# Idle transposes of the identity, early transposes in pairs, and one DMA queue for the last block but one

## The chip, the cores and the metric

The kernel runs on one core of one Trainium2 chip. Time is the device time of one execution in microseconds. A core has a matrix engine (TensorE; PE in the profile, its weight loads are PEld), a vector engine (VectorE, DVE), a scalar engine (ScalarE, ACT), GpSimd (POOL) and SyncE (SP). [...] SP, ScalarE and GpSimd can issue DMA transfers; an engine that issues one is occupied for that time.

## The reference: a sandwich of attention and a feed-forward layer

The input is 1024 rows of 512 numbers, all in fp32. What is computed, with 32 query heads and 8 key-value heads (groups) of width 128:

```python
q = (hidden_states @ w_q).reshape(B, S, Hkv, g, D)
k = (hidden_states @ w_k).reshape(B, S, Hkv, D)
v = (hidden_states @ w_v).reshape(B, S, Hkv, D)
scores = jnp.einsum('bqhgd,bkhd->bhgqk', q, k) * scale
scores = jnp.where(causal, scores, -jnp.inf)
probs = jax.nn.softmax(scores.astype(jnp.float32), axis=-1).astype(q.dtype)
attn = jnp.einsum('bhgqk,bkhd->bqhgd', probs, v)
return attn.reshape(B, S, Hq * D) @ w_o
...
x = x + _layernorm(_L0_attn_ref(_layernorm(x, axis=-1), ...), axis=-1)
x = x + _layernorm(_L0_ffn_ref(_layernorm(x, axis=-1), ...), axis=-1)
```

The second layer is a dense product with a bias plus 8 low-rank experts of rank 16, weighted by a router (softmax over 15 logits, the 8 largest, mapped to experts).

## The kernel before

**Tiles.** The rows are 8 tiles of 128. Work goes by blocks: a block is one group and one tile of rows (`t`), with the group's four heads, so 64 blocks, numbered by `i`. They come in pairs of neighbouring tiles. The last two groups are interleaved at the end so that rows finish one after another and the second layer can begin; the last pair, blocks 62 and 63, is the last group with `t` = 2 and 3.

**One block.** `scores` (L350) does a block in four sub-blocks: a matmul of queries and keys into PSUM (`s`), a causal mask added by VectorE (L370), the maximum (L372, `nmax`), the exponential on ScalarE (L377, `p`), the reciprocal and the scaling (L379, L380), and a VectorE transposition of 32 x 32 pieces into a tile `T` (L383). With few keys (`t` below 4) two sub-blocks share one tile of PSUM, and the second one's matmul waits for the first one's exponential. `to_keys` (L388) then moves `T` into a tile `K` with 16 DMA transfers, which carry the probabilities to the partitions of their keys. Two blocks later `weighted_values` (L398, `po`) multiplies values by them; later still come the output projection and, for the last group, the second layer.

**Order.** TensorE's instructions and all DMA issues are pinned to program order (`keep`). So are the input's normalisations on VectorE. The others (mask, maximum, exponential, copies, the subtractions of `combine_o` on GpSimd) are placed by a planner before the program runs; every engine's order is then fixed. While a block's scores run on VectorE and ScalarE, TensorE is fed with `then`: query projections of a later pair (`pq`), products of earlier blocks (`po`), output products and second-layer pieces, cut into four shares (L701 to L704).

**Start.** The eight tiles of x and the first weights come in on SP and ScalarE's queue (L152 to L162). `input_norms` (L236) normalises each tile: statistics on VectorE, a power on GpSimd, and a scaling on VectorE (L252). `input_turn` (L260) transposes one tile with four TensorE transposes into a PSUM bank (`ptx_x`) and copies it to `xnT` on ScalarE (L234). The first four tiles are turned ahead of the blocks, with the first value projections `project_v` (`pv`) between them; `project_k` (`pk`) and `project_q` (`pq`) follow; tiles 4 and 5 are turned inside block 0, tiles 6 and 7 inside block 1. `load_o` and `combine_o` load and prepare `w_o` for group 0 on SP and GpSimd. `bank` gives one of three PSUM banks in turn to the transposes and projections.

**End.** After block 63's scores a hand-written order (L713 to L731) finishes the last four tiles of rows. It begins with the output product of blocks 60 and 61, woven with `weighted_values` of block 62.

**Queues.** `to_keys` takes the engines that issue as `by`; `two` is SP and ScalarE, `two[:1]` is SP alone. Before the change blocks 62 and 63 use both, eight transfers each:

```python
to_keys(*blocks[i], by=two if i >= N - 2 else two[:1])
```

Of the kernel before, what the change touches and what calls it, by code (L numbers as in the profile page):

```python
# [15 lines left out]
P = 128  # L16
# [6 lines left out]
def kernel(  # L23
# [37 lines left out]
    KC = H // P  # L61
    QB = 512
    NQB = S // QB
    TPB = QB // P
# [23 lines left out]
    blocks = [(g, 2 * u + e) for g, u in pairs for e in range(2)]  # L88
    N = len(blocks)
    N2 = (G - 2) * NT  # L90

    def keep(ins):
        return tc.keep_in_program_order(ins)
# [4 lines left out]
    def transpose(*args):  # L98
        keep(nc.tensor.transpose(*args))

    def load(dst, src, by=nc.sync):
        keep(by.dma_start(dst, src))

    def turn_tile(kind, g, t):

        size = (NT - 1 + t % 2) * NSUB * P
        return turn.tile([P, size], F32, tag=f"{kind}{t % 2}", name=f"{kind}_{g}_{t}")
# [39 lines left out]
    two = (nc.sync, nc.scalar)  # L147
# [16 lines left out]
    ident = const.tile([P, P], F32, tag="ident", name="ident")  # L164
# [58 lines left out]
    def bank(name):  # L223
        return ps_m.tile([P, 512], F32, tag="pm", name=name)
# [4 lines left out]
    def transposed(dst, src, name):  # L229

        pt = bank(f"ptx_{name}")
        for c in range(KC):
            transpose(pt[:, ts(c, P)], src[:, ts(c, P)], ident)
        nc.scalar.copy(dst, pt.rearrange("p (c q) -> p c q", q=P))  # L234

    def input_norms(rows):  # L236

        mvs, rstds = {}, {}

        def begin(t):  # L240
            stats = small.tile([P, 6], F32, tag="stats", name=f"stats_x{t}")
            keep(nc.vector.bn_stats(stats, x_in[:, t, :]))
            mv = mvs[t] = small.tile([P, 2], F32, tag="mv", name=f"mv_x{t}")
            keep(nc.vector.bn_aggr(mv, stats))
            ve = small.tile([P, 1], F32, tag="ve", name=f"ve_x{t}")
            keep(nc.vector.tensor_scalar(ve, mv[:, 1:2], EPS, None, ALU.add))
            rstds[t] = small.tile([P, 1], F32, tag="rstd", name=f"rstd_x{t}")
            keep(nc.gpsimd.tensor_tensor(rstds[t], ve, neg_half, ALU.pow))

        def end(t):  # L250
            row = x_in[:, t, :]
            keep(nc.vector.tensor_scalar(row, row, mvs[t][:, 0:1], rstds[t], ALU.subtract, ALU.mult))  # L252

        for n, t in enumerate(rows):
            begin(t)
            if n:
                end(rows[n - 1])
        end(rows[-1])

    def input_turn(t):  # L260
        transposed(xnT[t // TPB][:, :, ts(t % TPB, P)], x_in[:, t, :], f"x{t}")
# [3 lines left out]
    def chained(get, terms, finish, cols=512):  # L265


        pm = []

        def piece(i):  # L270
            if i == 0:
                pm.append(get())
            lhsT, rhs = terms[i]()
            matmul(pm[0], lhsT, rhs, start=(i == 0), stop=(i == len(terms) - 1))
            if i == len(terms) - 1:
                finish(pm[0])

        return [(cols, lambda i=i: piece(i)) for i in range(len(terms))]

    def project_v(gv, t):  # L280
        def finish(pm):
            v = vs[gv, t] = act.tile([P, GV * D], F32, tag="v", name=f"v_{gv}_{t}", bufs=NT + 2)
            nc.scalar.copy(v, pm)

        def term(c):
            return xnT[t // TPB][:, c, ts(t % TPB, P)], weights["v", gv, c]

        return chained(
            lambda: bank(f"pv_{gv}_{t}")[:, : GV * D],
            [lambda c=c: term(c) for c in range(KC)],  # L290
            finish,
            GV * D,
        )

    def project_k(g, qb):
        def finish(pm):
            kT = kTs[g, qb] = act.tile([P, QB], F32, tag="kT", name=f"kT_{g}_{qb}", bufs=2 * NQB)
            nc.scalar.copy(kT, pm)

        def term(c):  # L300
            return weights["k", g][:, c, :], xnT[qb][:, c, :]

        return chained(
            lambda: bank(f"pk_{g}_{qb}"), [lambda c=c: term(c) for c in range(KC)], finish
        )
# [38 lines left out]
    def turn_view(w, t):  # L344
        n = t + 1
        return w[:, : n * NSUB * P].rearrange("p (b s k q) -> p b s k q", b=R, s=NSUB, k=n)
# [41 lines left out]
    def to_keys(g, t, by=(nc.sync,)):  # L388

        src = turned.pop((g, t))  # L390
        dst = keyed[g, t] = turn_view(turn_tile("K", g, t), t)
        for h in range(R):
            for b in range(NSUB):
                load(dst[ts(b, SQ), h, :, :, :], src[ts(h, SQ), b, :, :, :], by[b % len(by)])
# [102 lines left out]
    def reload_x(t):  # L497
        xt = state["x", t] = ffn.tile([P, H], F32, tag="x", name=f"xr_{t}", bufs=1)
        load(xt, x[ts(t, P), :])
# [78 lines left out]
    def ffn_store(t):  # L578
        load(out[ts(t, P), :], acc[t])


    def projections(i):


        g, t = blocks[i]
        q, other = [], []
        m = i // 2 + 1
        if i % 2 and m < len(pairs):
            q = project_q(*pairs[m])
        if i < N2:  # L590
            if t == 2:
                other += project_k(g, 1)
            if t == 6:
                other += project_k(g + 1, 0)
            if g == 0 and t < 2:
                other += [(P * KC, lambda n=n: input_turn(n)) for n in range(TPB + 2 * t, TPB + 2 * t + 2)]
                other += project_v(0, 2 + t)
            elif g % GV == 0 and (g or t >= TPB):
                other += project_v(g // GV, t)
        else:  # L600
            n = i - N2
            for k, what in ((0, (G - 1, 0)), (2, (G - 2, 1)), (3, (G - 1, 1))):
                if n == k:
                    other += project_k(*what)
            for t in {0: (0,), 1: (1,), 2: (2, 3), 3: (4, 5), 4: (6, 7)}.get(n, ()):
                other += project_v(g // GV, t)
        return q, other

    def loads(i):

        g, t = blocks[i]
        m = (i + 1) // 2 + 1
        if i % 2 == 0 and m < len(pairs):
            for j in range(2):
                load_q(pairs[m][0], j)
        if i < N2:
            if t == 3:
                load_k(g + 1)
            if t == 5 and g + 1 == G - 2:
                load_k(G - 1)  # L620
            if t == 6 and (g + 1) % GV == 0:
                for j in range(2):
                    load_v((g + 1) // GV, j)
            if t == 5:
                load_o(g + 1)
        elif i == N2 + 3:
            load_o(G - 1)
        elif i == N2 + 4:
            load_base("wk", (0, 1))
        elif i == N2 + 5:  # L630
            load_base("wv", (2, 3))

    def run(pieces):
        for _, f in pieces:
            f()
# [23 lines left out]
    input_norms(range(TPB))  # L659
    prepare_mask()  # L660
    input_norms(range(TPB, NT))
    for t in range(TPB):
        input_turn(t)
        if t < 2:
            run(project_v(0, t))
    run(project_k(0, 0))
    run(project_q(0, 0))
    load_o(0, nc.sync)
# [2 lines left out]
    def complete(i, *behind):  # L671


        for e in range(2):
            k = i - behind[e % len(behind)]
            if 0 <= k < N and k % 2 == e and blocks[k][0] == G - 1:
                return [blocks[k][1]]
        return []

    def attend(i):  # L680
        return weighted_values(*blocks[i])

    for i in range(N):
        loads(i)
        for t in complete(i, 2):
            reload_x(t)
        for t in complete(i, 7, 8):
            ffn_store(t)
        q, other = projections(i)
        pv = attend(i - 2) if i >= 2 else []  # L690
        o, o_pair, ends, begins = [], [], [], []
        for t in complete(i, 3):
            o = project_o(*blocks[i - 3])
        if i % 2 == 0 and i >= 4 and blocks[i - 4][0] < G - 1:
            o_pair = project_o_pair(*pairs[i // 2 - 2])
        for t in complete(i, 6, 7):
            ends = sum(ffn_out(t), [])
        for t in complete(i, 5):
            begins = ffn_router(t)

        then = begins[:1] + q + ends + o + weave(o_pair, begins[1:] + other + pv)  # L701
        for n in range(NSUB):
            scores(*blocks[i], n)
            run_share(then, n, NSUB)  # L704
        to_keys(*blocks[i], by=two if i >= N - 2 else two[:1])
        if i == NT:
            prepare_ffn()

        if i >= NT and blocks[i - 2][1] == 0 and blocks[i - 2][0] < G - 1:
            combine_o(blocks[i - 2][0])  # L710
# [62 lines left out]
```

## Time and profile before

| what | value |
|---|---|
| median of 3 runs | 1120.93 us (1120.46 to 1122.02) |
| the profiled execution's own time | 1155.51 us |
| its span, first to last instruction | 1153.7 us |
| mean granted TensorE clock in it | 0.943 of full speed |
| PE busy | 1116.4 us, 97% |
| DVE busy | 785.9 us, 68% |
| ACT busy | 308.6 us, 27% |
| POOL busy | 87.5 us, 8% |

The profile is one execution; its time is 3% above the median, so a sum made in its times has to be set against its own time first. A row of a timeline has the start in us, the duration, the engine, the line, the operation, what it writes and reads, how many such instructions are merged, and in brackets the idle time before it and what ended that. SPq and ACTq are DMA issues on SP and ScalarE; they are not counted as busy time. A fp32 product appears as two matmul instructions. A row of windows has the stretch, its length, the busy time of TensorE with its instructions, the granted clock, the busy share of the DMA engines and GB/s.

### The profile page before, as it was taken

How to read it: one execution, taken by the hardware profiler on the slowest of the kernel's cores; microseconds unless marked ns; L12 is line 12 of the kernel's file. 1: busy time of each engine (PE TensorE's matmuls, PEld its weight loads, DVE VectorE, ACT ScalarE, POOL GpSimd, SP SyncE). 2: the span in 40 equal slices, each digit the busy share in tenths (PEclk: the TensorE clock that was granted, in tenths of full speed). 3: DMA queues.
4: the chain of work that ended last, by engine and by line, in shares of the span. 5: the costliest groups of instructions: out<-in, count | busy, mean ns of one | idle time of the engine just before them, and what ended most of it. 6: DMA issues, size and time to landing. Idle time of an engine off the chain costs nothing.

```text
span 1153.7 us, 12792 instructions
## 1 busy us (share of the span) xinstructions
PE 1116.4 (97%) x3816; PEld 715.9 (62%) x3816; DVE 785.9 (68%) x1797; ACT 308.6 (27%) x729; POOL 87.5 (8%) x267
## 2 busy tenths in 40 slices
PE   6999999999999999999999999999999999999796
PEld 4666666666666666666676666666676546466353
DVE  4677657776577657786577656776447877877665
ACT  2433222322232222322232322322222322232210
POOL 5000002000010002000020002000020100000000
PEclk9999999999999999999999999999999999999898
DMA  6135232464126332454125432456224554443320
GB/s 202 39 98 139 64 83 57 122 154 90 26 73 163 74 83 55 113 143 110 28 73 142 95 81 51 123 133 152 65 57 138 143 133 95 110 114 78 82 64 28
DMA packets 79380, 111.82 MB, mean 97 GB/s; under 512 B 18176, under 2 KB 50960, under 8 KB 79312
## 3 DMA queue, kind: packets, MB, share of 16 engines
q1 hardware_dynamic: 53168, 81.99, 30.2%
q10 hardware_dynamic: 25808, 28.19, 8.0%
q0 software_dynamic: 336, 0.83, 0.2%
q8 instruction: 31, 0.51, 0.2%
q14 instruction: 37, 0.30, 0.1%
HBM read 33.34 MB, written 2.10 MB: 31 GB/s over the span
## 4 chain that ended last, share of the span: by engine, by line
PE 89%; DVE 7%; ACT 2%; issue 1%; DMA 1%; SPq 0%; POOL 0%; ACTq 0%; POOLq 0%; DVEq 0%
PE po L96 21%; PE s L96 20%; PE pq L96 18%; PE pv L96 5%; PE pk L96 5%; PE pa L96 4%; PE pe L96 4%; PE pO L96 2%; PE pb L96 2%; PE pd L96 2%; PE pc L96 2%; PE pf L96 2%; DVE T L383 1%; ACT p L377 1%; DVE nmax L372 1%; DVE p L380 1%
## 5 line engine op out<-in xcount | busy, mean ns | idle before, releaser
L377 ACT ACTIVATE p<-s,nmax 128x32 f32<-128x32 f32 (+31 forms) x256 | 179.3, 701 | 537.2 <-DVE nmax L372 462.0
L96 PE MATMUL s<-kT,qT 128*128 128x512 f32 (+15 forms) x768 | 285.4, 482 | 12.2 <-ACT p L377 11.6
L96 PE MATMUL po<-K,v 128*128 128x512 f32 x576 | 288.6, 618 | 0.0
L96 PE MATMUL pq<-xnT,wq 128*128 128x256 f32 x1024 | 244.3, 391 | 0.0
L96 PEld LDWEIGHTS s<-kT,qT 128*128 128x128 f32 x768 | 147.5, 194 | 149.3 <-issue 117.2
L96 PEld LDWEIGHTS pq<-xnT,wq 128*128 128x128 f32 x1024 | 196.5, 193 | 45.0 <-issue 17.3
L383 DVE STREAM_TRANSPOSE T<-p 128x128 f32<-128x128 f32 (+7 forms) x256 | 196.1, 773 | 15.8 <-DMA K<-T 2.7
L372 DVE TENSOR_REDUCE nmax<-s 128x1 f32<-128x32 f32 (+31 forms) x256 | 179.6, 701 | 6.1
L96 PEld LDWEIGHTS po<-K,v 128*128 128x128 f32 x576 | 110.6, 194 | 79.1 <-issue 68.8
L379 DVE RECIPROCAL rec<-total 128x1 f32<-128x1 f32 x256 | 40.9, 160 | 161.9 <-ACT p L377 160.4
L380 DVE TENSOR_SCALAR p<-p,rec 128x32 f32<-128x32 f32 (+31 forms) x256 | 129.4, 505 | 7.7
L370 DVE TENSOR_TENSOR s<-s,smask 128x32 f32<-128x32 f32 x256 | 49.0, 192 | 96.5 <-PE s L96 95.4
L375 POOL MEMSET p<- 128x96 f32 (+2 forms) x192 | 29.1, 152 | 892.1 <-DVE T L383 842.8
L96 PE MATMUL pv<-wv,xnT 128*128 128x256 f32 x256 | 72.5, 402 | 2.4 <-ACT xnT L234 1.4
L96 PE MATMUL pk<-xnT,wk 128*128 128x512 f32 x128 | 67.4, 618 | 0.7 <-ACT xnT L234 0.7
L320 ACT ACTIVATE qT<-pq 128x512 f32<-128x512 f32 x64 | 38.1, 596 | 109.1 <-PE pq L96 108.9
L96 PE MATMUL pa<-wo,attnT 128*128 128x256 f32 x224 | 64.0, 396 | 0.0
L404 ACT COPY attnT<-po 128x512 f32<-128x512 f32 x64 | 37.4, 585 | 83.5 <-PE po L96 76.9
L96 PEld LDWEIGHTS pv<-wv,xnT 128*128 128x128 f32 x256 | 49.7, 198 | 14.9 <-issue 3.2
L96 PEld LDWEIGHTS pa<-wo,attnT 128*128 128x128 f32 x224 | 41.8, 194 | 19.4 <-issue 14.6
L377 ACT ACTIVATION_READ_ACCUMULATOR p<-s,nmax 128x1 f32 x256 | 49.6, 194 | 0.0
L96 PE MATMUL pe<-wo,sums 128*128 128x256 f32 x112 | 33.4, 391 | 1.5 <-DVE acc L475 1.5
(100 smaller groups left out, 743.2 us busy)
## 6 DMA issues: line engine op xcount, KB each, us to landing
K<-T SPq DMA_DIRECT2D x128, 128.0 KB, 2.4
K<-T SPq DMA_DIRECT2D x128, 112.0 KB, 2.2
wq<-in_w_q_dram ACTq DMA_DIRECT2D x27, 512.0 KB, 5.2
K<-T SPq DMA_DIRECT2D x128, 96.0 KB, 2.2
K<-T SPq DMA_DIRECT2D x128, 80.0 KB, 2.1
K<-T SPq DMA_DIRECT2D x120, 64.0 KB, 2.0
wo<-in_w_o_dram ACTq DMA_DIRECT2D x28, 256.0 KB, 3.6
K<-T SPq DMA_DIRECT2D x120, 48.0 KB, 1.9
```

Source lines behind the costliest of these rows:

```text
L96: keep(nc.tensor.matmul(*args, **kw))
L320: nc.scalar.mul(qTs[g, u][:, :, j - 1 : j + 1, :].rearrange("p s h q -> p h s q"), pm[0].rearrange("p (h s q) -> p h s q", h=2, q=SQ), scale,)
L370: nc.vector.tensor_tensor(s[:, n - SQ : n], s[:, n - SQ : n], smask, ALU.add)
L372: nc.vector.tensor_reduce(nmax, s[:, :n], AX.X, ALU.max, negate=True)
L375: nc.gpsimd.memset(p[:, n:full], 0.0)
L377: nc.scalar.activation(p[:, :n], s[:, :n], AF.Exp, bias=nmax, accum_out=total)
L379: nc.vector.reciprocal(rec, total)
L380: nc.vector.tensor_scalar(p[:, :n], p[:, :n], rec, None, ALU.mult)
L383: nc.vector.transpose(turned[g, t][:, :, j, :, :].rearrange("p b k q -> p k b q"), p[:, :full].rearrange("p (k b q) -> p k b q", b=R, q=SQ),)
L404: nc.scalar.copy(o, po)
```

## The change

Three edits. First, before any tile is turned, TensorE transposes the identity matrix 20 times into a PSUM bank that nobody reads. Second, tiles 0 and 1 are both turned ahead of the first value projection, and tiles 2 and 3 ahead of the second. Third, only block 63 uses both queues in `to_keys`; block 62's 16 transfers are all issued by SP.

```diff
@@ -659,10 +659,16 @@
     input_norms(range(TPB))
     prepare_mask()
     input_norms(range(TPB, NT))
-    for t in range(TPB):
+
+    idle = bank("idle")
+    for n in range(20):
+        transpose(idle[:, ts(n % KC, P)], ident, ident)
+    for t in range(2):
         input_turn(t)
-        if t < 2:
-            run(project_v(0, t))
+    run(project_v(0, 0))
+    for t in range(2, TPB):
+        input_turn(t)
+    run(project_v(0, 1))
     run(project_k(0, 0))
     run(project_q(0, 0))
     load_o(0, nc.sync)
@@ -702,7 +708,7 @@
         for n in range(NSUB):
             scores(*blocks[i], n)
             run_share(then, n, NSUB)
-        to_keys(*blocks[i], by=two if i >= N - 2 else two[:1])
+        to_keys(*blocks[i], by=two if i == N - 1 else two[:1])
         if i == NT:
             prepare_ffn()
 
```

## The prediction

> **What bounds the kernel now.** The page's fourth part, the chain that ended last, comes first:
>
> ```profile
> PE 89%; DVE 7%; ACT 2%; issue 1%; DMA 1%; SPq 0%; POOL 0%; ACTq 0%; POOLq 0%; DVEq 0%
> ```
>
> TensorE carries the end. A table by stretches of 10 us shows it busy 10.00 of 10 in nearly all rows from 70 to 1080 us. The middle only shifts; the change must act in the first 35 us or after 1080. Next, the timeline of the end (start, duration, engine, line, operation, idle before):
>
> ```profile
> 1082.88 5.32 ACTq L102 DMA_DIRECT2D K<-T  x8
> 1083.04 0.59 DVE L372 TENSOR_REDUCE nmax<-s 128x1 f32<-128x416 f32 x1
> 1084.43 0.17 DVE L524 TENSOR_REDUCE nmaxr<-lg 128x1 f32<-128x15 f32 x1
> 1088.33 0.61 ACT L377 ACTIVATE p<-s,nmax 128x416 f32<-128x416 f32 x1 [6.88 <-DMA K<-T]
> 1089.06 0.16 DVE L379 RECIPROCAL rec<-total 128x1 f32<-128x1 f32 x1 [4.46 <-ACT p L377]
> 1089.08 1.86 PE L96 MATMUL s<-kT,qT 128*128 128x448 f32 x2 [6.31 <-ACT p L377]
> 1096.38 1.16 PE L96 MATMUL s<-kT,qT 128*128 128x512 f32 x2 [1.20 <-ACT p L377]
> ```
>
> Block 62 has just been turned. ScalarE issues 8 of its 16 transfers, in order, for 5.3 us; block 63's first exponential, whose maximum was ready at 1083.63, waits behind them, and TensorE idles 6.3 us. From 1096.38 TensorE is dense to 1126. Then the start:
>
> ```profile
> 8.31 3.78 PE L96 MATMUL pv<-wv,xnT 128*128 128x256 f32 x8 [0.68 <-ACT xnT L234]
> 13.62 2.06 PE L96 MATMUL pv<-wv,xnT 128*128 128x256 f32 x8 [0.67 <-ACT xnT L234]
> 20.99 7.36 PE L96 MATMUL pq<-xnT,wq 128*128 128x256 f32 x32
> 28.20 0.55 DVE L252 TENSOR_SCALAR K_x<-K_x,mv_x,rstd_x 128x512 f32<-128x512 f32 x1 [0.44 <-POOL rstd_x L248]
> 29.48 0.20 DVE L370 TENSOR_TENSOR s<-s,smask 128x32 f32<-128x32 f32 x1 [0.73 <-PE s L96]
> 29.96 0.58 ACT L234 COPY xnT<-ptx_x 128x512 f32<-128x512 f32 x1 [0.97 <-PE ptx_x L99]
> 30.44 0.29 ACT L377 ACTIVATE p<-s,nmax 128x32 f32<-128x32 f32 x1
> ```
>
> The same 8 matmuls take 3.78 us, then 2.06: TensorE starts slow. VectorE's last row normalisation ends at 28.75, just ahead of the first mask addition. Last, windows (length, PE busy, granted clock, DMA):
>
> ```profile
> 945.51:948.92 3.41, 0.83 (x3) 0.95 0.77 200
> 948.92:952.33 3.41, 3.41 (x7) 0.50 0.90 199
> 27.32:30.73 3.41, 1.91 (x11) 0.95 0.00 0
> 1133.24:1136.65 3.41, 1.20 (x6) 0.95 0.00 0
> 1136.65:1140.07 3.42, 2.78 (x10) 0.50 0.20 77
> ```
>
> A window 24% or 35% busy is followed by one at half clock; 56% is not.
>
> [...]
>
> **The end.** Removed: 8 issues on ScalarE at block 62 (5.32 us). Added: 8 on SP. The exponential starts 0.12 after its maximum (as the next one does: 1091.81+0.61 to 1092.54), at 1083.75. VectorE's reciprocal then waits for the router maximum ahead of it (1084.60): 1084.64 in place of 1089.06, 4.4 earlier. The router exponential moves from 1088.93 to 1084.72, 4.2. From there to 1096.38 VectorE and ScalarE hand on to each other without a gap of their own (mask addition 1091.50, exponential 1092.54, reciprocal 1093.30, transposition 1093.98, mask addition 1094.62, exponential 1095.58), so the last score matmul comes 4.3 earlier, at 1092.0.
> What the cover costs: SP issues 16 in place of 8. An earlier block's row in the timeline of SP, and the page's sixth part (KB each, us from issue to landing), price it:
>
> ```profile
> 1046.64 10.02 SPq L102 DMA_DIRECT2D K<-T  x16
> K<-T SPq DMA_DIRECT2D x120, 48.0 KB, 1.9
> ```
>
> That is 0.63 for an issue. From 1082.9 the last of 16 starts 15 x 0.63 later, at 1092.4, and lands at 1094.3. The first reader, the product of values and weights of block 62, stood at 1100.06 and comes to 1095.7: hidden with 1.4 to spare. Behind the 16 on SP wait a store (1087.91, read by nobody) and block 63's 8 transfers, wanted at 1097.4; SP is free at 1093.6. Block 63 keeps both queues.
> What is late next: TensorE. It starts block 63's second score at 1084.5 warm, finishes all it has by 1088.9 (0.8 for the score, 1.8 for 4 `po`, 0.84, 0.9), then idles 3.1 us until 1092.0. A 3.41-us window on that gap is under about 45% busy for E, its end, from 90.7 to 93.5 (2.8 of 3.41, 80%). Then dense work runs at half clock for 2.2 to 3.4 us: 1.1 to 1.7 lost, taken as 1.6. End: 4.3 - 1.6 = +2.7, bounds +2.6 to +4.4; +5.7 if VectorE's work is re-ordered (the transfers cap it: 1100.06 - 1094.3).
>
> **The start.** Added: 20 transposes of the identity, which is ready at 1.45. A slow one takes 0.278 (1.11 for 4), a fast one 0.134 (1.07 for 8): 5.6 us slow, to 7.0, so the first real ones (6.52) are up to 0.5 late; less if the clock rises on the way. Their bank is one of three; its next user is `pv` 0, on TensorE itself. The transposes read no new data and nobody reads their bank. Their cost is hidden either way: row 1 is normalised only at 8.80. Moved: turn 1 to 8.85-9.4, `pv` 0 to 9.4-11.3, turns 2 and 3 (rows ready 10.81, 12.11) to 12.7, `pv` 1 to 14.6, `pk` (3.86) to 18.2, `pq` to 25.4: 3.0 earlier than 28.36; if transposes don't warm the clock, `pv` 0 runs slow to 13.7 and `pq` ends at 27.4, 1.0 earlier. Weights have landed (issue plus time to landing: `wk` 2.2 + 7.5, the later `wq` 4.2 + 8.4).
> But the mask addition stands on VectorE behind row 7's normalisation, at 28.75, which follows rows 4 to 6 and their powers on GpSimd; those stand among four subtractions on `wo` (1.3 each), whose load GpSimd awaits until 19.44. None of that touches TensorE, so it stays. So 29.48 becomes 28.78 (0.7), and row 4's copy on ScalarE, now long done, leaves the first exponential at 29.25 in place of 30.44: +1.2. In the timed runs TensorE is faster (below), so less is left there: +0.2 to +1.2, taken as +0.7.
> What is late next: between 25.4 and 29.7 TensorE has 0.8 us of work, so a window ending between 28 and 31 (8 in 10) drops the clock. Dense work begins at 31.9; the half-clock window ends between 31.4 and 34.4 (0 to 1.2 lost), the scores and turns inside lengthen the chain by up to 0.6 (4 transposes of 0.278 in place of 0.134), and a window that began idle may be followed by a second slow one (1.7 lost then). So 0 to 2.3; taken as 0.8, since most of the slow window lies where TensorE waits anyway. Start: 0.7 - 0.8 = -0.1, bounds -2.1 to +1.2. PSUM, TensorE work and loads elsewhere: unchanged.
>
> **Sum.** 2.7 - 0.1 = 2.6. The profiled execution took 1155.51 us (span 1153.7) at clock 0.943; the median is 1120.93, 3% less, by estimate a clock near 0.98. What moves is ScalarE, VectorE and SP time, so I subtract it unscaled: 1118.3.
>
> **Rivals.**
> *No clock drop at the end* (the gap straddles two windows; the start comes out at +0.3): 4.3 + 0.3 = 4.6, 1116.3. For: 2 in 10 phases, and windows of 56% that stayed fast. Against: a gap of 3.1 us.
> *Both ends go cold in full*: 4.3 - 1.7 - 1.4 (0.7 gained, 2.1 lost) = 1.2, 1119.7. For: both gaps, 3.1 us and 4.3 us with 0.8 of work, are about as long as a window. Against: the costly phases at the start are a third of all.
> *The transfers on one queue become the wait* (slower): place, the first `po` of block 62; TensorE waits there if the last lands after 1095.7, eats the 2.6 at 1098.3, and is 0.2% slower at 1100.6: an issue every 1.05 us ((1100.6 - 1.9 - 1082.9) / 15), giving 1120.93 + 2.24 = 1123.2. Against: 0.63 in the run of 16.
> *The change doesn't act*: the planner that places the unpinned VectorE and ScalarE instructions puts another wait ahead of the exponential: 1120.9. Against: all it needs is ready at 1083.63.
>
> **Chances.** Forecast 50% (own range 1117.2 to 1119.5; about two thirds of it below 1118.7), no drop 25%, both cold 17%, transfers 5%, nothing 3%. What a measurement here tells from no change is about 0.2%, 2.24 us. Faster: 0.34 + 0.25 = 0.59; same: 0.16 + 0.17 + 0.03 = 0.36; slower 0.05. Range: 1116.0 to 1120.6 takes in all but the transfers and the outer bounds.
>
> **What would show it.** Right: no ScalarE issues at block 62; the 128x416 exponential within 0.2 us of its maximum; 16 SP issues over 10 us; the last score 4.3 us nearer to block 62's turning; a gap of 3 us before it and a 0.50 window after. At the start: `pq` ending near 25.4, mask addition directly behind row 7's normalisation, a gap of 3 us. Wrong: a TensorE wait on `K` at block 62; `pv` 0 still 3.8 us (transposes don't warm); row normalisations at other times.

## The result, and the profile after

The changed kernel takes 1117.82 us (median of 14 runs, 1113.84 to 1119.95), the kernel before 1119.99 us (14 runs of the same sessions, 1118.48 to 1122.28). The ratio is 0.9974, with a 95% interval of 0.9965 to 0.9983: 2.9 us faster, between 1.9 and 3.9. (The ratio and its interval come from all the runs; the two medians by themselves are 2.2 us apart.) The forecast was 1118.3 us and 2.6 us faster.

The profiled execution of the changed kernel took 1115.06 us (span 1113.1) at a mean granted clock of 0.991; it is 2.8 us under the median and so one of the quicker ones. The profile before had been taken at 0.943, so stretches are compared below by what moved within them, and the kernels of the experiments, all near 0.99, are compared with each other.

The chain that ended last, by engine, in the changed kernel:

```profile
PE 81%; DVE 10%; DMA 3%; ACT 2%; SPq 1%; POOL 1%; issue 1%; ACTq 0%; POOLq 0%; DVEq 0%
```

TensorE still carries the end, but DMA has come up from 1% to 3% and VectorE from 7% to 10%: the chain now runs for a while through transfers (its largest piece of that kind is 3.01 us, from 55.18 to 58.19 us, in block 3). The timeline of the changed kernel's end:

```profile
1048.64 0.56 DVE L383 STREAM_TRANSPOSE T<-p 128x384 f32<-128x384 f32 x1
1049.39 0.59 DVE L372 TENSOR_REDUCE nmax<-s 128x1 f32<-128x416 f32 x1
1050.10 0.61 ACT L377 ACTIVATE p<-s,nmax 128x416 f32<-128x416 f32 x1 [2.56 <-POOL rstd_h L220]
1050.85 1.02 PE L96 MATMUL s<-kT,qT 128*128 128x448 f32 x2 [2.01 <-ACT p L377]
1051.71 3.08 PE L96 MATMUL po<-K,v 128*128 128x512 f32 x4
1056.13 0.20 DVE L370 TENSOR_TENSOR s<-s,smask 128x32 f32<-128x32 f32 x1 [0.99 <-PE s L96]
1058.38 1.12 PE L96 MATMUL s<-kT,qT 128*128 128x512 f32 x2 [1.43 <-ACT p L377]
1061.93 1.02 PE L96 MATMUL po<-K,v 128*128 128x512 f32 x2
```

The 128x416 exponential starts 0.12 us after its maximum (1049.39 + 0.59), with no issue ahead of it. TensorE waits 2.01 us for it in place of 6.31. From the end of block 62's turning (1048.64 + 0.56 = 1049.20) to block 63's last score it is 9.18 us, where it was 13.53 (1082.85 to 1096.38): 4.35 us less. The slower clock of the profile before does not make this difference: in the six kernels below that keep two queues for block 62, at full clock, the same stretch is 13.5 to 13.7 us. The first product of block 62, at 1061.93, waits for nothing. SP's own timeline shows its 16 issues there, inside an unbroken run that ends at 1059.28:

```profile
1033.11 26.17 SPq L102 DMA_DIRECT2D K<-T  x32
```

The windows of that stretch (length, PE busy, granted clock):

```profile
1048.83:1052.24 3.41, 1.40 (x5) 1.00 0.18 43
1052.24:1055.66 3.42, 3.42 (x6) 0.50 0.35 84
1055.66:1059.07 3.41, 1.98 (x5) 1.00 0.32 77
```

A window 41% busy is followed by one at half clock, and that one, which ends at 1055.66, is over before the last score (1058.38).

The start of the changed kernel:

```profile
1.50 3.77 PE L99 MATMUL idle<-ident 128*128 128x128 f32 x20 [1.50 <-POOL ident masks.py:199]
10.22 3.62 PE L96 MATMUL pv<-wv,xnT 128*128 128x256 f32 x8
14.98 1.89 PE L96 MATMUL pv<-wv,xnT 128*128 128x256 f32 x8
20.14 7.07 PE L96 MATMUL pq<-xnT,wq 128*128 128x256 f32 x32
28.53 0.55 DVE L252 TENSOR_SCALAR K_x<-K_x,mv_x,rstd_x 128x512 f32<-128x512 f32 x1 [0.44 <-POOL rstd_x L248]
28.81 0.58 ACT L234 COPY xnT<-ptx_x 128x512 f32<-128x512 f32 x1 [0.97 <-PE ptx_x L99]
28.99 0.19 DVE L370 TENSOR_TENSOR s<-s,smask 128x32 f32<-128x32 f32 x1
29.44 0.29 ACT L377 ACTIVATE p<-s,nmax 128x32 f32<-128x32 f32 x1
```

and its windows there:

```profile
4.35:7.77 3.42, 1.58 (x12) 1.00 1.07 356
7.77:11.18 3.41, 1.87 (x7) 0.50 1.08 358
11.18:14.59 3.41, 3.41 (x12) 0.50 1.06 329
```

The 20 transposes took 3.77 us; at the pace of the first four in the profile before (1.11 us) it would have been 5.6, so by this estimate the clock rose while they ran. It fell again: after them TensorE waited 1.22 us for row 0 and 2.16 us for row 1, the window was 46% busy, the next two stand at 0.50, and the first value projection took 3.62 us, the very thing that the transposes had warmed up for. The query projections end at 27.2, not 25.4. The mask addition stands directly behind row 7's normalisation, as forecast.

### The profile page after: what moved, and what is told of

It is laid out like the page before. It is cut to its first block, busy times and chain, and to the rows that moved or that the text cites. A ratio compares the mean times of both kernels' runs of the same rounds, so it can differ in the third digit from the quotient of the medians.

```text
span 1113.1 us, 12830 instructions
## 1 busy us (share of the span) xinstructions
PE 1076.3 (97%) x3836; PEld 705.6 (63%) x3836; DVE 783.5 (70%) x1797; ACT 308.0 (28%) x729; POOL 87.2 (8%) x267
## 4 chain that ended last, share of the span: by engine, by line
PE 81%; DVE 10%; DMA 3%; ACT 2%; SPq 1%; POOL 1%; issue 1%; ACTq 0%; POOLq 0%; DVEq 0%
PE po L96 20%; PE s L96 18%; PE pq L96 16%; PE pk L96 4%; PE pe L96 4%; PE pv L96 4%; PE pa L96 4%; DVE T L383 2%; PE pd L96 2%; PE pc L96 2%; DVE nmax L372 2%; PE pb L96 2%; DMA K<-T 2%; ACT p L377 2%; PE pf L96 1%; SPq L102 1%
## 5 line engine op out<-in xcount | busy, mean ns | idle before, releaser
L96 PE MATMUL s<-kT,qT 128*128 128x512 f32 (+15 forms) x768 | 275.8, 468 | 12.5 <-ACT p L377 11.7
L96 PE MATMUL po<-K,v 128*128 128x512 f32 x576 | 276.9, 595 | 0.0
L96 PEld LDWEIGHTS s<-kT,qT 128*128 128x128 f32 x768 | 144.6, 191 | 143.5 <-issue 107.2
L96 PE MATMUL pq<-xnT,wq 128*128 128x256 f32 x1024 | 234.9, 379 | 0.0
L96 PEld LDWEIGHTS pq<-xnT,wq 128*128 128x128 f32 x1024 | 193.1, 190 | 38.7 <-issue 16.5
L96 PE MATMUL pv<-wv,xnT 128*128 128x256 f32 x256 | 69.8, 389 | 1.7 <-ACT v L283 1.4
L96 PE MATMUL pk<-xnT,wk 128*128 128x512 f32 x128 | 64.5, 593 | 0.0
L404 ACT COPY attnT<-po 128x512 f32<-128x512 f32 x64 | 37.3, 583 | 71.5 <-PE po L96 63.9
```

The source lines that it names most:

```text
L96: keep(nc.tensor.matmul(*args, **kw))
L404: nc.scalar.copy(o, po)
```

## Experiments

Differences are ratios to the kernel before, in the same session, times its median (1119.3 to 1119.9 us). Two theories were held against each other first. A: the gain is ScalarE freed at block 62, and the start gives nothing. B: the gain comes from the start.

**Only the third edit.**

```diff
-        to_keys(*blocks[i], by=two if i >= N - 2 else two[:1])
+        to_keys(*blocks[i], by=two if i == N - 1 else two[:1])
```

> Only the third edit: block 62 issues on SP alone, the start as before. Theory A (the gain is ScalarE freed at block 62; the clock decides how much of it is kept): 2.6 to 4.4 us faster than before; last score of block 63 comes 9.0 to 9.5 us after block 62's turning ends, in place of 13.5. Rival B (the gain comes from the start, the end only fills waiting): within 1 us of before.

Measured: 1115.97 us, ratio 0.9965 (0.9952 to 0.9979): 3.9 us faster. The last score comes 9.17 us after block 62's turning (1047.74 to 1056.91). A holds. The interval, 2.4 to 5.4 us, is wide; the profiles narrow it. From block 62's turning to the last instruction the six kernels with two queues for it take 68.4 to 69.8 us, and the six with one queue and 16 transfers 63.9 to 64.6 us: about 5 us less. So this edit alone is at least as good as the whole change.

**Only the first two edits.** The new start, with the old line of `to_keys`.

> Only the first two edits: idle transposes and turns in pairs, block 62 on two queues as before. Theory A: between 2 us slower and 1.2 us faster, about the same; first mask addition directly behind row 7's normalisation. Rival B: 2 us or more faster.

Measured: ratio 1.0018 (1.0009 to 1.0026): 2.0 us slower. B falls. A's band reached to 2 us slower, so A is not refuted, but it had named no cause for a loss of this size. The next two runs divide it.

**Only the second edit.**

```diff
-    for t in range(TPB):
+    for t in range(2):
         input_turn(t)
-        if t < 2:
-            run(project_v(0, t))
+    run(project_v(0, 0))
+    for t in range(2, TPB):
+        input_turn(t)
+    run(project_v(0, 1))
```

> Only the second edit: turns in pairs, no idle transposes. Theory A: TensorE waits for row 1 until 8.8 to 9.3 us, then works slow until a window is full; query projections end about where they did (28.4 us, within 1), so within 0.7 us of before. Rival B (grouping saves waits of TensorE): 1 us or more faster.

Measured: ratio 0.9995 (0.9987 to 1.0003): no difference, as A had it for the time. The first value projection was slow, as A had it (3.52 us), but A's detail was wrong: the query projections end at 25.6 us, 2 to 3 us earlier. They gain nothing, and the timeline and the windows show where it goes:

```profile
26.30 0.41 PE L96 MATMUL s<-kT,qT 128*128 128x32 f32 x2 [0.69 <-ACT qT L320]
29.85 0.69 PE L96 MATMUL s<-kT,qT 128*128 128x64 f32 x2 [2.67 <-ACT p L377]
```

```profile
26.09:29.50 3.41, 0.88 (x6) 1.00 0.00 0
29.50:32.92 3.42, 3.07 (x12) 0.50 0.02 5
```

TensorE comes early, waits 2.67 us for the first exponential, which hangs on row 7, and goes on at half clock (0.50 from 29.50 to 32.92) behind a window 26% busy. Block 0's transfers are first issued at 35.81 us, against 35.22 in the kernel with only the third edit, which has the old start: the lead is gone before block 1. This is the price that the forecast had named for the start.

**Only the first edit.** The 20 transposes, then the old order.

> Only the first edit: 20 transposes of the identity, then turns and value projections in the old order. Theory A: the clock rises during the transposes (as in the changed kernel's profile, 1.0 from 4.35 us) and mostly falls again in the wait for row 0 and row 1; first value projection between 1.9 and 3.8 us depending on the phase; whole kernel within 1 us of before. Rival C (transposes do not raise the clock[...]): first value projection always 3.7 us, kernel within 0.3 us of before.

Measured: ratio 1.0015 (1.0007 to 1.0022): 1.7 us slower. C falls: the first value projection was slow, as C had it (3.57 us in this profile), but the 20 transposes took 3.90 us, not 5.6, and the four of row 0 behind them 0.66 us, against 1.12 in the kernel with only the third edit: the transposes had raised the clock. A's "within 1 us" falls too. The place is block 3, in the timelines of the kernel with only the third edit (first fence, no idle transposes) and of this one (second fence):

```profile
57.03 0.71 DVE L383 STREAM_TRANSPOSE T<-p 128x512 f32<-128x512 f32 x1 [1.34 <-DMA K<-T]
62.52 1.12 PE L96 MATMUL s<-kT,qT 128*128 128x512 f32 x2 [1.31 <-ACT p L377]
```

```profile
57.83 0.71 DVE L383 STREAM_TRANSPOSE T<-p 128x512 f32<-128x512 f32 x1 [2.73 <-DMA K<-T]
63.32 2.07 PE L96 MATMUL s<-kT,qT 128*128 128x512 f32 x2 [2.69 <-ACT p L377]
```

`T` has one buffer for even and one for odd tiles. Block 3's first transposition overwrites block 1's, so VectorE waits until SP has issued blocks 0 and 1 (32 issues of 0.63 us without a pause, begun at 34.6 here) and the last has landed. Up to block 2 this kernel runs 0.58 us ahead of the other (last turning of block 2 ends at 54.41 against 54.99); at block 3 it is 0.80 behind. The lead itself is not what makes the wait longer, since SP began its issues earlier by as much (34.63 against 35.22). What changed is the landing. The DMA view of 54 to 58 us, kernel with the third edit only, then this one:

```profile
K<-T SPq DMA_DIRECT2D x3, 32.0 KB, 2.4
```

```profile
q8 instruction: 1, 0.02, 1.6%
...
K<-T SPq DMA_DIRECT2D x2, 32.0 KB, 3.1
```

Block 1's last transfers needed a median of 3.1 us to land, against 2.4 (2.7 in the kernel with eight idle transposes; 1.9 is the median of all 128 transfers of this size in the profile before). The very last, the one that VectorE waits for, was issued by estimate at 54.16 us here and at 54.75 in the other kernel (31 x 0.63 behind the first); VectorE goes on 3.7 and 2.3 us later, and these 1.4 us are the whole growth of its wait (1.34 to 2.73). In the same 4 us this kernel alone of the two has an instruction fetch of 16 KB (q8). The changed kernel has one there too, and the DMA views of it and of the kernel before show the slow landings where the fetch is: at 54 to 58 us the changed kernel has the fetch, and block 1's last transfer landed 3.5 us after its issue, against 2.3 in the kernel before, which has none from 50 to 62; at 62 to 66 us it is the kernel before that has the fetch, and its transfers of block 2 needed a median of 2.4 us, against 2.0 in the changed one. Then the clock fell:

```profile
59.25:62.66 3.41, 1.38 (x7) 1.00 0.31 74
62.66:66.07 3.41, 2.75 (x5) 0.50 0.36 85
66.07:69.48 3.41, 3.41 (x6) 0.50 0.07 16
69.48:72.90 3.42, 3.42 (x16) 1.00 0.29 68
```

The window with the wait is 40% busy, and two at half clock follow, with 6.2 us of work in them: about 3 us lost. From block 2 to block 5 this execution falls back by 4.4 us on the other one: 1.4 by the landing, 3.0 by the clock. A wait of this length did not always cost the clock. In the changed kernel's own profile TensorE waits 2.89 us at block 3, but two windows share this wait (58.96 to 62.38 us, 54% busy, and 62.38 to 65.79, 61%), and both and the next stand at 1.00. That the fetch delays the landing and the wait costs the clock became the theory that the next runs test, against D: the transposes cost in some other way.

**Eight idle transposes.** `range(8)` in place of `range(20)`.

> The first edit alone with 8 idle transposes in place of 20. Theory A: 20 of them add 40 TensorE instructions, which brings a 16 KB instruction fetch from 64 us to 55.5 us, into the last transfers of block 1, for which VectorE waits at block 3; TensorE's wait there grows from 1.3 to 2.7 us and the clock falls. With 8 the fetch comes at about 60 us, VectorE's wait ends by 57.1, TensorE waits 1.9 us or less there, and the kernel is within 0.7 us of before. Rival D (the idle transposes cost through something else, in proportion to their number or by being there): 0.7 to 1.7 us slower.

Measured: ratio 0.9996 (0.9987 to 1.0005): no loss. VectorE waits 1.63 us at block 3 (until 57.54), TensorE 1.6. No fetch is in its DMA view of 54 to 58 us, and the last three transfers of block 1 needed a median of 2.7 us. D falls, if narrowly: its 0.7 us lies just outside the interval. So the loss goes with the fetch and the wait; that the fetch came at 60 us, as the arithmetic of instructions had it, is not shown.

**A tile of its own for block 1's turned probabilities.** They go into memory that is first written later, so block 3 need not wait for them.

```diff
         size = (NT - 1 + t % 2) * NSUB * P
+        if kind == "T" and (g, t) == (0, 1):
+            return sums_o[3].rearrange("p a n -> p (a n)")
```

> The kernel before, with block 1's turned probabilities in memory of their own (a sum that is first written later), so that block 3 need not wait for block 1's transfers. Theory A: VectorE's wait for K at block 3 and TensorE's 1.3 us there go; 0.5 to 1.5 us faster than before, less if a later wait on SP's issues takes it. Rival D: no statement (same as before if that wait is no part of the chain).

Measured: ratio 0.9978 (0.9971 to 0.9984): 2.5 us faster, more than the 1.3 us of the wait. The timeline:

```profile
56.04 0.71 DVE L385 STREAM_TRANSPOSE T<-p 128x512 f32<-128x512 f32 x1
61.52 1.13 PE L96 MATMUL s<-kT,qT 128*128 128x512 f32 x2
```

Neither VectorE nor TensorE waits there now. The rest is not accounted for. The mean granted clock was higher in this kernel's runs (median of 21: 0.993) than in those of the kernel before (0.991, median of 35), but no profile here shows what raised it.

**The same with the 20 idle transposes.**

> The same with the 20 idle transposes. Theory A: with the wait at block 3 away their loss goes too: between 0.8 us faster and 0.5 us slower than the own-tile kernel without them. Rival D: 1.7 us slower than that kernel, as it was with the shared tile.

Measured: ratio 0.9970 (0.9959 to 0.9980), against 0.9978 without them: 0.9 us faster, but the intervals overlap, so no difference is shown. The loss of 1.7 us is gone although the fetch is still there between 54 and 59 us (and block 1's last four transfers still needed a median of 3.3 us to land). D falls: what the idle transposes cost is the wait at block 3. Its start:

```profile
6.54 0.66 PE L99 MATMUL ptx_x<-ident,K_x 128*128 128x128 f32 x4 [0.51 <-DVE K_x L254]
8.17 1.99 PE L96 MATMUL pv<-wv,xnT 128*128 128x256 f32 x8 [0.97 <-ACT xnT L236]
29.70 0.48 PE L96 MATMUL s<-kT,qT 128*128 128x64 f32 x2 [2.65 <-ACT p L379]
```

Here the first value projection took 1.99 us, not 3.6, and the lead was given back in a wait of 2.65 us and slow work behind it: the four matmuls of `pv` from 31.20 us took 1.97 us, the next four 1.03.

**The third edit and the own tile together**, old start.

> Block 62 on SP alone, and the own tile for block 1; no idle transposes, old order of turns. Theory A: both gains add, 3.9 + 0.5 to 1.5, so 4.4 to 5.4 us faster than before, ahead of the changed kernel by 2 or more.

Measured: 1111.88 us, ratio 0.9928 (0.9916 to 0.9941): 8.1 us faster. That is more than 3.9 + 2.5, but the third edit's own 3.9 us was uncertain: against the kernel with the own tile alone, timed in the same session, the third edit is worth 5.6 us here, close to the 5 us that the profiles show. In its profile the last score comes 8.11 us after block 62's turning (1045.57 to 1053.68), with no window at half clock there; in the three profiles with such a window, this edit and 16 transfers, it was 9.17 to 9.18. This does not explain a surplus, since from the last score to the end it then took 56.3 us, and those three 54.7 to 55.4.

**Block 62's transfers cut in two**, on the kernel just shown: `parts=2` for block 62.

```diff
-                load(dst[ts(b, SQ), h, :, :, :], src[ts(h, SQ), b, :, :, :], by[b % len(by)])
+                for s in range(parts):
+                    half = ts(s, NSUB // parts)
+                    load(dst[ts(b, SQ), h, half, :, :], src[ts(h, SQ), b, half, :, :], by[b % len(by)])
```

> Block 62 on SP alone with an own tile for block 1, as before, but each of block 62's 16 transfers cut into two: 32 issues of 24 KB. It prices the cover of the 16. Theory A (16 issues are hidden with 1.3 us to spare before the first product of block 62, 12.7 us after its turning): 32 land 31 x 0.63 + 1.9 = 21.5 us after it, TensorE waits 8 to 9 us there, and the kernel is 7 to 9 us slower than the one with 16. Rival E (those transfers have much more slack than that): within 3 us of it.

Measured: 1127.15 us, ratio 1.0061 (1.0047 to 1.0075), 14.9 us slower than with 16 transfers. The waits and the windows:

```profile
PE po L96 <- DMA K<-T: 10.1, 1, 10.1
```

```profile
1065.75:1069.17 3.42, 0.00 (x0) 0.50 0.39 94
1069.17:1072.58 3.41, 2.15 (x3) 0.50 0.64 200
1072.58:1075.99 3.41, 3.41 (x9) 0.50 0.43 101
```

TensorE waits exactly at the first product of block 62, for 10.1 us, then works 5.6 us in windows at 0.50, half of which is lost by estimate: 10.1 + 2.8 = 12.9. From the last score to the end this profile is 12.7 us longer than that of the kernel with 16. The rest of the difference between the two profiles lies at the start, which the edit does not touch: here the second value projection was slow too (3.78 us in place of 1.99), and block 0 was turned 2.9 us later. A had 7 to 9: the landing was right (21.5 us after the turning forecast, 21.9 measured), but in this faster kernel the product comes 11.7 us after the turning, not 12.7, and the clock was left out. With 16 issues the last starts at 9.5 us and lands near 11.4: hidden, with some 0.3 us to spare.

**Block 63 on SP alone too**: `by=two[:1]` for all.

> The same with block 63 on SP alone too (16 issues of 64 KB). Theory A (issues on ScalarE cost only where an exponential waits behind them; after block 63 nothing urgent does, and its product comes 14 us after its turning): within 0.5 us of the kernel with two queues for block 63. Rival F (any issue on ScalarE near the end costs): 1 us or more faster than it.

Measured: ratio 0.9939 (0.9924 to 0.9953), against 0.9928 with both queues: 1.2 us slower, outside A's 0.5, but the intervals overlap and the two were timed in different sessions. In the profiles, from block 62's turning to the end, the two kernels take the same 64.4 us. F falls. Block 62's issues on ScalarE cost, with an exponential behind them; block 63's do not.

**The subtractions on `w_o` pinned behind the normalisations**, on the kernel with the third edit and the own tile.

```diff
-        nc.gpsimd.tensor_tensor(dst, p, q, ALU.subtract)
+        keep(nc.gpsimd.tensor_tensor(dst, p, q, ALU.subtract))
```

> Block 62 on SP alone, own tile for block 1, and the four subtractions on w_o pinned behind the row normalisations on GpSimd; no idle transposes, old order. Theory A: rows 4 to 7 are normalised by 19 us in place of 28.8, the first mask addition follows the first score directly; 0 to 1 us faster than without the pinning.

Measured: ratio 0.9948 (0.9936 to 0.9961), against 0.9928 (0.9916 to 0.9941) without the pinning: 2.2 us slower, but the intervals overlap and the sessions differ, so a loss is not shown; a gain is not there. The rows did come earlier:

```profile
20.16 1.49 DVE L254 TENSOR_SCALAR K_x<-K_x,mv_x,rstd_x 128x512 f32<-128x512 f32 x1 [0.44 <-POOL rstd_x L250]
28.52 0.20 DVE L372 TENSOR_TENSOR s<-s,smask 128x32 f32<-128x32 f32 x1 [6.87 <-PE s L96]
```

Row 7 is done at 21.6 us, and the mask addition waits for TensorE alone. In this order TensorE is the later one, so nothing is won. The profiled execution (span 1110.5) shows no loss of 2 us either (1110.0 without the pinning).

**The whole change with the own tile and the pinning.**

> The whole change with the own tile and the pinning. Theory A: now neither row 7's normalisation nor block 1's transfers take the start's gain back; TensorE's earlier arrival (query projections ending 24 to 27 us) is kept: 0.5 to 3 us faster than the kernel of the same build without the two start edits. Rival D (the start edits gain nothing even where nothing waits): within 0.5 us of it, or slower.

Measured: 1111.02 us, ratio 0.9924 (0.9910 to 0.9937): 2.7 us faster than the same build without the start edits. The time falls in A's band and not in D's, but A's path is not shown: the query projections end at 27.5 us, not between 24 and 27, and 27.4 in the kernel without the start edits; block 0 is turned 0.14 us later, not earlier. Against the unpinned kernel with the old start (0.9928) the start edits are worth nothing that shows. So whether they gain where nothing waits behind them stays open. One candidate is the spread of the old start: in the six profiles with it at full clock, block 0 is turned at 34.6 to 37.4 us, latest where the second value projection was slow too (3.78 us); in the five with 20 idle transposes at 34.6 to 35.9. No run isolates this. This kernel and the unpinned one are the fastest here, both some 8 us ahead of the kernel before and 5 to 6 ahead of the change.

## Why the prediction was right, and where it was not

**The end, shift.** Forecast 4.3 us from the turning of block 62 to the last score; 4.35 in the profile. The exponential 0.12 after its maximum, SP's 16 issues in 10 us and no wait at the first product of block 62 are as worked out. That the shift came out so near is partly luck, because two things that the forecast's sum did not have cancel. The planner put most of the router's small VectorE operations (1090.61 to 1091.58 before) behind the next mask addition and not ahead of it: in the four profiles without a half-clock window there, the last score comes 8.1 us after the turning, a shift of 5.4 us, as the bound "+5.7 if VectorE's work is re-ordered" had allowed. And the half-clock window, where it falls there, takes 1.1 us of this back. Cutting the transfers in two put the wait exactly where the rival about transfers had placed it; with 16 it does not act.

**The end, clock.** Forecast: a gap of 3.1 us before the last score, then 1.6 us lost in dense work. Mis-sized. That a window can end anywhere on the gap, and so its chances, was an estimate. The gap was 2.07 us where the clock held, because the last score came earlier, and 1.43 in the changed kernel, where the half-clock window came one gap earlier: there TensorE was still at the work ahead of the last score, and VectorE waited 0.99 us for it. In the dense work nothing was lost: from the last score to the end the kernels with one queue and 16 transfers take 54.7 to 56.3 us, those with two also 54.7 to 56.3. The edit alone measured 3.9 us (2.4 to 5.4), with the own tile 5.6, and about 5 in the profiles, against 2.7.

**The start.** Forecast -0.1 us, measured 2.0 us slower. The gate of row 7 was right, and so was the drop of the clock behind it, shown by the kernel with the turns in pairs. What failed is the sentence that says what is late next at the start: it stopped at block 1. Block 3's wait for block 1's transfers stood in the trace before, in VectorE's row, and was not looked for:

```profile
58.08 0.71 DVE L383 STREAM_TRANSPOSE T<-p 128x512 f32<-128x512 f32 x1 [1.10 <-DMA K<-T]
```

It does not take back a lead by itself, since SP's issues begin earlier with the lead. But in the profiles with 20 idle transposes and the shared tile block 1's last transfer landed later (3.5 us after its issue in the changed kernel, 2.3 in the kernel before), and VectorE's wait was 2.73 us with the first edit alone and 2.92 in the changed kernel. In the first of these TensorE's window there was 40% busy and the clock fell; in the second its windows were 54% and 61% busy and it held. Pairing alone cost nothing, idle transposes alone 1.7, both 2.0.

**The sum.** 2.7 - 0.1 = 2.6 forecast; +3.9 and -2.0 measured apart, which makes 1.9, and 2.9 together (1.9 to 3.9). The total was near by luck: two errors of opposite sign, 1.2 us at the end (some 2 by the profiles) and 1.9 us at the start, nearly cancelled.

## What to carry to other kernels

Eight DMA issues on ScalarE, 5.32 us, were paid here by the exponential that stood behind them, and by TensorE with 6.31 us: read the next instruction on an engine before spreading transfers over queues, and price the single queue by issues times the time of one (16 x 0.63 us here). A lead won at the start has to be followed through several blocks, reuse of single buffers above all: ask at each wait on another resource whether what it waits for moves with the lead. Warming TensorE up ahead of waits was mostly undone by them: in four of five profiles with 20 idle transposes the first value projection still took 3.57 to 3.62 us, and 1.99 in the fifth. A longer wait later can cost the lost clock as well: about 3 us behind the wait of 2.69 us in the kernel with only the first edit, nothing behind that of 2.89 in the changed one.

## What was unexpected in the hardware

Transposes alone raised TensorE's clock, fp32 transposes of the identity as this kernel makes them. In the five kernels with 20 of them they took 3.77 to 4.53 us, where 20 at the pace of the first four in the profile before (1.11 us) would take 5.6; and the four transposes of row 0 that follow took 0.65 to 0.66 us, against 1.11 to 1.12 without idle transposes. In the changed kernel the window from 4.35 us, 2.9 us after the first of them began, stands at 1.00.

The stretches at half clock within the profiles of the kernel before and of the changed kernel last 3.41 or 6.83 us, one or two of the windows above. By the modelled ends of the matmuls, the windows there at the higher clock (0.95 and 1.00) that were followed by half clock were 0%, 21%, 24% and 35% busy before, 14%, 41%, 46% and 47% after; two more above, in the kernels with only the second and only the first edit, 26% and 40%. The least busy that were followed by the higher clock were 49% (1093.20 to 1096.62 us, changed kernel), 54% (changed) and 56% (before). From half clock, one 0% busy was followed by another at half clock in the kernel before, one 55% busy in the changed kernel (7.77 to 11.18 us), one 63% in the kernel with block 62's transfers in two (1069.17 to 1072.58) and one 81% in the kernel with only the first edit (62.66 to 66.07); one 81% busy in the kernel before (1136.65 to 1140.07) and those of 94% and 100% were followed by the higher clock. These are readings of a few windows, not a limit.

An instruction fetch of 16 KB coincided with slow landings of block 1's transfers. In the changed kernel the last one landed 3.5 us after its issue, with a fetch between 55.5 and 57.1 us; in the kernel before it took 2.3, with no fetch from 50 to 62. The kernels with only the first edit and with both start edits have a fetch from 50 to 62 us too, that with own tile and idle transposes from 54 to 59; those with only the second and only the third edit have none from 50 to 62, that with eight idle transposes none from 54 to 58. That the fetch delayed the landings is argued from this coincidence, and from the kernel before being the slower one at 62 to 66 us (2.4 against 2.0 us), where it has the fetch; it was not isolated. What decides where such a fetch falls is not shown.
